# Attention and feed-forward on one core: the first pass over the keys begins with half of them, and projection blocks are cut in pieces of two matmuls

## The chip, the cores and the metric

The kernel runs on one NeuronCore of one Trainium2 chip. The metric is the device time of one execution in microseconds (us); each kernel is timed in several runs, and the median is given. A profile comes from one execution of its own.

## The reference, cut to what matters

Two sequences (B = 2) of T = 1024 rows of width D = 512 go through attention with 32 query heads and 8 key/value heads of width 16, a residual and a layer norm, then through a gated feed-forward of width 1408, a residual and a second layer norm. All is float32.

```python
Q = (x @ Wq.T + bq).reshape(b, t, HQ, HD).transpose(0, 2, 1, 3)
K = (x @ Wk.T + bk).reshape(b, t, HKV, HD).transpose(0, 2, 1, 3)
V = (x @ Wv.T + bv).reshape(b, t, HKV, HD).transpose(0, 2, 1, 3)
Q, K = _rope(Q, K)
K, V = jnp.repeat(K, G, axis=1), jnp.repeat(V, G, axis=1)
scores = jnp.einsum('bhqd,bhkd->bhqk', Q, K) / np.sqrt(HD)
w = jax.nn.softmax(scores, axis=-1)
attn = jnp.einsum('bhqk,bhkd->bhqd', w, V)
x = layernorm(x + attn.transpose(0, 2, 1, 3).reshape(b, t, D) @ Wo.T + bo)
out = layernorm(x + (silu(g) * u) @ down_w.T * down_s)      # g, u: gate and up of x
```

## The kernel before, in words

**Units and passes.** A unit `u` is one sequence `b`, one half `qh` of its queries (512) and one key head `g` with its four query heads; there are 32 units. Each unit is worked in eight steps. **Pass A** (`max_pass`, L325) multiplies queries by keys and takes each row's maximum: one step is one tile `t` of 128 queries against one half of 512 keys, for four heads. For each head two matmuls (`QH` and `QL`, the high and low part of the query) fill one PSUM bank, and VectorE reduces it to a column of `mx` (L341). When the eight steps of a unit are through, `max_rows` sends the maxima through DRAM into `mt`. **Pass B** (`exp_pass`, L362) forms the scores again, transposed, adds the negated maximum by a third matmul, and ScalarE takes the exponential (L378); `av` (L389) multiplies by V.

**Lead and loop.** Pass A runs LEAD = 12 steps ahead of pass B. These twelve steps stand alone in a first loop, called the lead below (`for n in range(LEAD)`, L623). After it comes the main loop over `c`, two steps of each pass a turn. The order of its instructions is written out by hand in three lists: `WITH_FILL` starts with `F`, which takes one item from the list `fill` and issues it; `NO_FILL` has no such item. While the first sequence's units run, `fill` holds 22 items, one a turn: two and four Q blocks of the first sequence, and sixteen items for the second sequence. After them turns run with `NO_FILL` until the projection and feed-forward items of the first quarter of rows become due, at turn c = 35. Those due turns are counted in c, not in time.

**A projection block.** `qk_block(b, half, m)` (L235) makes 128 columns of Q or K (m = 4 is K) for 512 rows: four program matmuls, which the profile records as eight, into one bank. Then ScalarE adds the bias (`q`, L256), GpSimd multiplies by the cosine (`t1`, L258), VectorE swaps the halves of each head (`rot`, a stream shuffle, L261), and `rot` times the sine, the sum, the high part and the low part follow (L262 to L265). With `fast=True` these are on VectorE and ScalarE and follow at once; otherwise GpSimd does them, one step later by `after(1, rest)`, and the two stores to DRAM are issued two steps after that. `rot` and `t1` have one buffer each. `prep(u)` (L310) loads a unit's keys `KS` and queries `QH`, `QL` back from DRAM. Each engine, and SyncE's queue of transfers, takes its instructions in the order of the program here (`tc.manual_schedule()`, L607).

**The start.** Eight tiles of x are loaded, then weights. Four tiles are turned by `x_turn` (L221), the rotation tables by `rope_turn` (L200, whose first instruction copies the table out to `rep` on VectorE, L203), then the other four tiles. Then come K of both halves, the first Q block, V of both halves (L292, L299), `prep(0)` and `prep(1)`, and the lead:

```python
qk_block(0, 0, D // P, fast=True)
qk_block(0, 1, D // P, fast=True)
qk_block(0, 0, 0, fast=True)
for half in range(NH):
    v_block(0, half)
prep(0)
prep(1)
```

One more Q block is issued whole in the lead, at n = 2 (L632). PSUM has four banks for pass A (`ps_a0`) and four for all else (`ps_q`) up to the end of the lead.

Of the kernel before, what the change touches and what calls it, by code (L numbers as in the profile page):

```python
# [7 lines left out]
F32 = mybir.dt.float32  # L8
I32 = mybir.dt.int32
F32R = mybir.dt.float32r  # L10
# [6 lines left out]
P = 128  # L17
B, T, D = 2, 1024, 512
HQ, HKV, HD = 32, 8, 16
G = HQ // HKV  # L20
E = 32
INTER = 1408
NT = T // P
# [3 lines left out]
QK = D + HKV * HD  # L27
KV = D + HKV * HD
HALF = 512
NH = T // HALF  # L30
TH = HALF // P
# [15 lines left out]
def attn_ffn_kernel(tc, x, wqkv, bqkv, wo, bo, rope, wg, wu, wd, gs, us, ds, out):  # L47
    nc = tc.nc
# [9 lines left out]
    ap3 = pool("ap3", 3)  # L58
    ap4 = pool("ap4", 4)
    wp = pool("wp", RING, side="right")  # L60
    qp1 = pool("qp1", side="right")
# [7 lines left out]
    def bank(name, shape=(P, HALF)):  # L69
        p, tag = psf[0]  # L70
        return p.tile(list(shape), F32, tag=tag, name=name)
# [8 lines left out]
    rope_sb = qp1.tile([P, NT, 2, HD], F32, name="rope_sb")  # L80
# [3 lines left out]
    def load_x(b, t):  # L84
        if b == 0:
            if t % TH == 0:
                XS["first"] = ap3.tile([P, TH, D], F32, tag="prob", name="xs0")
            XS[b, t] = XS["first"][:, t % TH, :]
        else:
            XS[b, t] = qp4.tile([P, D], F32, tag="xs", name="xs")  # L90
        nc.sync.dma_start(out=XS[b, t], in_=x[b, t * P : (t + 1) * P, :])

    def load_wqkv(n0, n1):
        nc.sync.dma_start(out=wqkv_sb[:, :, n0:n1], in_=wqkv[:, :, n0:n1])

    nc.sync.dma_start(out=rope_sb, in_=rope)
    for t in range(TH):
        load_x(0, t)
    for t in range(TH, NT):
        load_x(0, t)  # L100
    load_wqkv(D, KV)
    nc.sync.dma_start(out=bcol, in_=bqkv[:, 0:QK].rearrange("o (m p) -> p (o m)", p=P))
    load_wqkv(0, P)
    load_wqkv(KV, W)
    nc.sync.dma_start(out=bv_sb, in_=bqkv[:, KV:W].to_broadcast([P, W - KV]))
    load_wqkv(P, D)
# [19 lines left out]
    qT, kT = [], []  # L126
# [68 lines left out]
    XT, QB = {}, {}  # L195
    swap = [(i ^ (HD // 2)) for i in range(E)]
    cosT = qp1.tile([P, T], F32, name="cosT")
    sinT = qp1.tile([P, T], F32, name="sinT")

    def rope_turn():  # L200

        rep = qp1.tile([P, NT * 2, P // HD, HD], F32, name="rep")
        nc.vector.tensor_copy(  # L203
            rep,
            rope_sb.rearrange("p t s d -> p (t s) d")
            .unsqueeze(2)
            .to_broadcast([P, NT * 2, P // HD, HD]),
        )
        for i, tab in enumerate((cosT, sinT)):
            for half in range(NH):  # L210
                pt = bank("pt")
                for t in range(TH):
                    row = rep[:, (half * TH + t) * 2 + i, :, :]
                    nc.tensor.transpose(
                        pt[:, t * P : (t + 1) * P],
                        row.rearrange("p h d -> p (h d)"),
                        ident,
                    )
                nc.scalar.copy(tab[:, half * HALF : (half + 1) * HALF], pt)
# [15 lines left out]
    def qk_block(b, half, m, c0=0, c1=NC, fast=False):  # L235

        if c0 == 0:
            QB["p"] = bank("pq")
        pq = QB["p"]
        for c in range(c0, c1):  # L240
            nc.tensor.matmul(  # L241
                pq,
                wqkv_sb[:, c, m * P : (m + 1) * P],
                XT[b, half][:, c, :],
                start=c == 0,
                stop=c == NC - 1,
            )
        if c1 < NC:
            return
        ns = slice(half * HALF, (half + 1) * HALF)  # L250
        q = qp2.tile([P, HALF], F32, tag="q", name="q")
        rot = qp1.tile([P, HALF], F32, tag="rot", name="rot")
        t1 = qp1.tile([P, HALF], F32, tag="t1", name="t1")
        hi = qp2.tile([P, HALF], F32R, tag="hi", name="hi")
        lo = qp2.tile([P, HALF], F32R, tag="lo", name="lo")
        nc.scalar.activation(q, pq, AF.Identity, bias=bcol[:, m : m + 1])  # L256
        e = nc.vector if fast else nc.gpsimd
        nc.gpsimd.tensor_tensor(t1, q, cosT[:, ns], ALU.mult)  # L258

        def rest():  # L260
            nc.vector.stream_shuffle(rot, q, swap)  # L261
            e.tensor_tensor(rot, rot, sinT[:, ns], ALU.mult)  # L262
            e.tensor_tensor(t1, t1, rot, ALU.add)
            (nc.scalar.copy if fast else nc.gpsimd.tensor_copy)(hi, t1)
            e.tensor_tensor(lo, t1, hi.bitcast(F32), ALU.subtract)  # L265

        def store():
            for i, h in enumerate((hi, lo)):
                if m == D // P:
                    nc.sync.dma_start(  # L270
                        out=kT[b].rearrange("(p r) n -> p r n", r=2)[:, i, ns], in_=h.bitcast(F32)
                    )
                else:
                    nc.sync.dma_start(
                        out=qT[b][half, i, m * 2 * P : (m + 1) * 2 * P, :].rearrange(
                            "(p r) n -> p r n", r=2
                        ),
                        in_=h.bitcast(F32).unsqueeze(1).to_broadcast([P, 2, HALF]),
                    )

        if fast:
            rest()
            store()
        else:
            after(1, rest)
            after(3, store)

    def v_block(b, half):
        pv = bank("pv", (P, TH, HKV * HD))
        for t in range(TH):  # L290
            for c in range(NC):
                nc.tensor.matmul(  # L292
                    pv[:, t, :],
                    XT[b, half][:, c, t * P : (t + 1) * P],
                    wqkv_sb[:, c, KV:W],
                    start=c == 0,
                    stop=c == NC - 1,
                )
        nc.vector.tensor_tensor(  # L299
            vas[b][:, half * TH : (half + 1) * TH, :, :, 0],  # L300
            pv.rearrange("p t (g d) -> p t g d", d=HD),
            bv_sb.rearrange("p (g d) -> p g d", d=HD).unsqueeze(1).to_broadcast([P, TH, HKV, HD]),
            ALU.add,
        )
# [2 lines left out]

    KS, QH, QL, MX = {}, {}, {}, {}

    def prep(u):  # L310
        b, qh, g = UNITS[u]
        KS[u] = ap3.tile([P, T], F32R, tag="KS", name="KS")
        QH[u] = ap3.tile([P, HALF], F32R, tag="QH", name="QH")
        QL[u] = ap3.tile([P, HALF], F32R, tag="QL", name="QL")
        for j in range(G):
            nc.sync.dma_start(
                out=KS[u][j * E : (j + 1) * E, :].bitcast(F32), in_=kT[b][g * E : (g + 1) * E, :]
            )
        for i, op in enumerate((QH[u], QL[u])):
            nc.sync.dma_start(out=op.bitcast(F32), in_=qT[b][qh, i, g * P : (g + 1) * P, :])  # L320

# [2 lines left out]

    def max_pass(n, j, i):  # L325
        u, s = divmod(n, US)
        t, half = divmod(s, NH)
        if u not in MX:
            MX[u] = ap2.tile([P, TH, G, NH], F32, tag="mx", name="mx")
        r = slice(j * E, (j + 1) * E)  # L330
        if i == 0:
            PA[n, j] = ps_a[0].tile([P, HALF], F32, tag="pa", name="pa")
        nc.tensor.matmul(  # L333
            PA[n, j],
            (QH, QL)[i][u][r, t * P : (t + 1) * P],
            KS[u][r, half * HALF : (half + 1) * HALF],
            start=i == 0,
            stop=i == 1,
        )
        if i == 1:  # L340
            nc.vector.tensor_reduce(MX[u][:, t, j, half : half + 1], PA.pop((n, j)), AX.X, ALU.max)  # L341
# [233 lines left out]
        after(1 if q == LASTQ else 2 if now[0] >= STEPS else 5, store)  # L575


    fill = [lambda a=(0, half, m): qk_block(*a) for half, m in ((0, 2), (0, 3))]
    fill += [lambda m=m: qk_block(0, 1, m) for m in range(QK // P - 1)]

    def two_turns(t):
        for i in (t, t + 1):
# [8 lines left out]
    fill = [(0, f) for f in fill]  # L591
# [18 lines left out]
    for t in range(TH):  # L610
        x_turn(0, t)
    rope_turn()
    for t in range(TH, NT):
        x_turn(0, t)
    qk_block(0, 0, D // P, fast=True)
    qk_block(0, 1, D // P, fast=True)
    qk_block(0, 0, 0, fast=True)
    for half in range(NH):
        v_block(0, half)
    prep(0)  # L620
    prep(1)
    ps_a = [ps_a0]
    for n in range(LEAD):  # L623
        now[0] = n - LEAD
        for a in "0a 1a 0b 1b 2a 3a 2b 3b".split():
            max_pass(n, int(a[0]), "ab".index(a[1]))
        for f in later.pop(now[0], ()):
            f()
        if n % US == US - 1:
            max_rows(n // US)  # L630
        if n == 2:
            qk_block(0, 0, 1)  # L632
        if n == 7:
            prep(2)
    for t in range(4):
# [28 lines left out]
    for c in range(STEPS // 2):  # L664
# [11 lines left out]
        for s in NO_A if alone else WITH_FILL if has_fill else NO_FILL:  # L676
# [7 lines left out]
            n = 2 * c + int(s[-1])  # L684
# [5 lines left out]
            j, i = int(s[1]), "abc".index(s[2])  # L690
# [7 lines left out]
        u, s = divmod(2 * c + 1, US)  # L698
# [4 lines left out]
        if c == QS // 2 - 6:  # L703
# [9 lines left out]
                out=wd_sb.bitcast(F32), in_=wsd[2 * NF : PIECES].rearrange("f p n -> p f n")  # L713
# [159 lines left out]
```

## Time and profile before

| | us |
|---|---|
| median of three runs (lowest to highest) | 1245.93 (1244.38 to 1246.58) |
| time of the profiled execution | 1244.49 |
| its span | 1242.4 |
| TensorE busy | 1170.1 (94%) |
| VectorE busy | 872.4 (70%) |
| ScalarE busy | 704.7 (57%) |
| GpSimd busy | 354.1 (29%) |
| first matmul of pass A starts at | 38.10 |
| first block of the main loop starts at | 74.03 |

The span is the time from the first to the last instruction on the profiler's clock, and all places in time below are counted from its start. "Busy" counts the time in which an engine has an instruction in work; a matmul's end is modelled. The granted clock is the share of TensorE's full clock. The mean clock of the whole execution is 0.969.

### The profile page before, as it was taken

To read this page: it belongs to the slowest core of one execution; us is meant where nothing else is said; L and a number is where in the kernel's file an instruction comes from. 1 tells how busy PE (TensorE), PEld (TensorE's weight loads), DVE (VectorE), ACT (ScalarE), POOL (GpSimd) and SP (SyncE) were. 2 spreads that over 40 slices of the span, in tenths; PEclk is the share of its full clock that TensorE was granted. 3 is DMA by queue.
4 is the path that set the end of the run, shared out by engine and by line. 5 is a ranking of instruction groups with operands and counts; after the bars stand their busy time and mean duration, and the time that the engine had idled before them with its cause. 6 is when DMAs were issued, how large, how long until landed. Compare 5 with 4: busy or idle time off the path is not lost.

```text
span 1242.4 us, 22712 instructions
## 1 busy us (share of the span) xinstructions
PE 1170.1 (94%) x8784; PEld 606.5 (49%) x8784; DVE 872.4 (70%) x1492; ACT 704.7 (57%) x1300; POOL 354.1 (29%) x340
## 2 busy tenths in 40 slices
PE   7799999999799999999999999999999999999876
PEld 5344435454344454545444454546444454455664
DVE  4578898878677878785568878784867878703324
ACT  2026757566555766765446676763547776762350
POOL 3126351530103222224421222225331222245321
PEclk9679999999899999999999999999999999999897
DMA  5457776433411222221312222221212222111420
GB/s 159 130 190 252 249 233 237 155 132 122 135 44 61 79 79 81 93 78 52 99 48 67 82 92 84 84 78 44 79 60 87 78 78 79 45 61 43 136 60 36
DMA packets 82291, 126.80 MB, mean 102 GB/s; under 512 B 15873, under 2 KB 29442, under 8 KB 82050
## 3 DMA queue, kind: packets, MB, share of 16 engines
q1 hardware_dynamic: 82178, 125.30, 31.6%
q8 instruction: 71, 1.16, 0.4%
q14 instruction: 42, 0.34, 0.1%
HBM read 80.43 MB, written 36.44 MB: 94 GB/s over the span
## 4 chain that ended last, share of the span: by engine, by line
PE 62%; DVE 21%; POOL 5%; DMA 4%; issue 3%; ACT 3%; SPq 1%; POOLq 0%; DVEq 0%; ACTq 0%
PE pb L370 14%; PE pv L389 13%; DVE mx L341 12%; PE pa L333 11%; PE pg L504 10%; PE pq L241 5%; PE pd L546 5%; PE py L463 3%; DVE den L417 3%; POOL z L532 1%; DVE st L448 1%; DMA fl<-red 1%; POOL xq L561 1%; POOL ys L560 1%; DVE z L523 1%
## 5 line engine op out<-in xcount | busy, mean ns | idle before, releaser
L341 DVE TENSOR_REDUCE mx<-pa 128x1 f32<-128x512 f32 x1024 | 643.2, 681 | 187.8 <-PE pa L333 185.6
L378 ACT ACTIVATE prob<-pb 128x512 f32<-128x512 f32 x1024 | 544.5, 599 | 274.1 <-PE pb L370 263.0
L333 PE MATMUL pa<-KS,QH 32*128 32x512 f32 x1024 | 365.8, 470 | 41.7 <-DVE mx L341 23.8
L333 PE MATMUL pa<-KS,QL 32*128 32x512 f32 x1024 | 349.1, 432 | 0.0
L370 PE MATMUL pb<-QH,KS 32*128 32x512 f32 x1024 | 321.7, 477 | 1.0 <-ACT prob L378 1.0
L389 PE MATMUL pv<-prob,va 128*32 128x512 f32 x2048 | 275.5, 610 | 0.0
L370 PE MATMUL pb<-QL,KS 32*128 32x512 f32 x1024 | 270.6, 423 | 0.0
L370 PE MATMUL pb<-mt,ones 32*128 32x512 f32 x1024 | 254.5, 395 | 0.0
L333 PEld LDWEIGHTS pa<-KS,QH 32*128 32x128 f32 x1024 | 154.0, 186 | 168.7 <-DVE mx L341 144.2
L532 POOL TENSOR_TENSOR z<-pus,z 128x512 f32<-128x512 f32 x44 | 56.2, 1277 | 462.7 <-ACT pus L529 462.7
L370 PEld LDWEIGHTS pb<-QH,KS 32*128 32x128 f32 x1024 | 134.9, 182 | 82.5 <-issue 48.9
L370 PEld LDWEIGHTS pb<-QL,KS 32*128 32x128 f32 x1024 | 125.6, 184 | 85.6 <-issue 85.5
L333 PEld LDWEIGHTS pa<-KS,QL 32*128 32x128 f32 x1024 | 163.3, 188 | 5.4 <-DMA QL<-qT 0.5
L370 PEld LDWEIGHTS pb<-mt,ones 32*128 32x128 f32 x1024 | 140.6, 184 | 23.7 <-issue 15.9
L504 PE MATMUL pg<-x1h,wt 128*128 128x512 f32 x352 | 146.5, 416 | 0.7 <-ACT x1h L493 0.7
L504 PE MATMUL pg<-x1l,wt 128*128 128x512 f32 x352 | 139.5, 396 | 0.3 <-DVE x1l L494 0.3
L389 PEld LDWEIGHTS pv<-prob,va 128*32 128x32 f32 x2048 | 40.8, 108 | 93.9 <-issue 82.7
L504 PEld LDWEIGHTS pg<-x1h,wt 128*128 128x128 f32 x352 | 67.1, 191 | 38.0 <-issue 12.8
L546 PE MATMUL pd<-wd_sb,hh 128*128 128x512 f32 x176 | 71.8, 408 | 10.8 <-ACT hh L534 10.2
L241 PE MATMUL pq<-xT,wqkv_sb 128*128 128x512 f32 x160 | 76.7, 626 | 0.0
L504 PEld LDWEIGHTS pg<-x1l,wt 128*128 128x128 f32 x352 | 67.2, 191 | 13.1 <-DVE x1l L494 0.8
L546 PE MATMUL pd<-wd_sb,hl 128*128 128x512 f32 x176 | 70.5, 401 | 0.2 <-DVE hl L535 0.2
(80 smaller groups left out, 976.5 us busy)
## 6 DMA issues: line engine op xcount, KB each, us to landing
wt<-wsd SPq DMA_DIRECT2D x88, 256.0 KB
KS<-kT SPq DMA_DIRECT2D x128, 128.0 KB
wsd<-sr SPq DMA_DIRECT2D x33, 256.0 KB
qT<-hi SPq DMA_DIRECT2D x16, 512.0 KB
qT<-lo SPq DMA_DIRECT2D x16, 512.0 KB
QH<-qT SPq DMA_DIRECT2D x32, 256.0 KB
QL<-qT SPq DMA_DIRECT2D x32, 256.0 KB
xs<-in_x_dram SPq DMA_DIRECT2D x16, 256.0 KB
```

Of the source, the lines that this page charges most:

```text
L241: nc.tensor.matmul(pq, wqkv_sb[:, c, m * P : (m + 1) * P], XT[b, half][:, c, :], start=c == 0, stop=c == NC - 1,)
L333: nc.tensor.matmul(PA[n, j], (QH, QL)[i][u][r, t * P : (t + 1) * P], KS[u][r, half * HALF : (half + 1) * HALF], start=i == 0, stop=i == 1,)
L341: nc.vector.tensor_reduce(MX[u][:, t, j, half : half + 1], PA.pop((n, j)), AX.X, ALU.max)
L370: nc.tensor.matmul(PB[n, j], ones[r, :] if i == 2 else KS[u][r, kc * P : (kc + 1) * P], (QH[u], QL[u], mts[u % 2])[i][r, :], start=i == 0, ...
L378: nc.scalar.activation(prob[:, j, :], PB.pop((n, j)), AF.Exp, scale=SCALE)
L389: nc.tensor.matmul(PV[u][j * E : (j + 1) * E, :], vas[b][:, kc, g, :, :].rearrange("p d o -> p (d o)"), prob[:, j, :], start=done == 0, st ...
L417: after(min(k + 1, TH - 1), lambda ns=ns: nc.vector.reciprocal(den[:, ns], den[:, ns]))
L448: nc.vector.bn_stats(st, row)
L463: nc.tensor.matmul(py, NUM[q, c][:, t * P : (t + 1) * P], wo_sb[:, c, :], start=c == 0, stop=c == NC - 1,)
L504: nc.tensor.matmul(p, w[:, c, :], x1[:, c, :], start=c == 0 and k == 0, stop=c == NC - 1 and k == 1,)
L532: nc.gpsimd.tensor_tensor(z, pus, z, ALU.mult)
L546: nc.tensor.matmul(pd, h[:, f, t * P : (t + 1) * P], wd_sb[:, f, :], start=f == 0 and k == 0, stop=f == NF - 1 and k == 1,)
```

## The change

The second four tiles of x are loaded after the first weights. `rep` is copied before anything else on VectorE. The K block of the first half and the first Q block are issued right after `rope_turn`, ahead of the second four tiles; `prep` can load half of the keys, and the first unit's keys are loaded in two halves. Pass A takes all four query tiles against the first half of the keys, then against the second. V of the first half stays ahead of the lead; V of the second half and four Q blocks (one of them stood whole at n = 2 before, three stood in `fill`) are cut in two pieces each, and one piece is issued after each of the steps n = 1 to n = 10 of the lead. `fill` has 19 items in place of 22.

```diff
     for t in range(TH):
         load_x(0, t)
-    for t in range(TH, NT):
-        load_x(0, t)
     load_wqkv(D, KV)
     nc.sync.dma_start(out=bcol, ...)
     load_wqkv(0, P)
+    for t in range(TH, NT):
+        load_x(0, t)
     load_wqkv(KV, W)
...
+    rep = qp1.tile([P, NT * 2, P // HD, HD], F32, name="rep")
+    nc.vector.tensor_copy(rep, ...)
     def rope_turn():
-        rep = qp1.tile([P, NT * 2, P // HD, HD], F32, name="rep")
-        nc.vector.tensor_copy(rep, ...)
...
-    def v_block(b, half):
-        pv = bank("pv", (P, TH, HKV * HD))
-        for t in range(TH):
+    def v_block(b, half, t0=0, t1=TH):
+        if t0 == 0:
+            QB["v"] = bank("pv", (P, TH, HKV * HD))
+        pv = QB["v"]
+        for t in range(t0, t1):
...
+        if t1 < TH:
+            return
         nc.vector.tensor_tensor(
...
-    def prep(u):
+    def prep(u, n0=0, n1=T):
         b, qh, g = UNITS[u]
-        KS[u] = ap3.tile([P, T], F32R, tag="KS", name="KS")
+        if n0 == 0:
+            KS[u] = ap3.tile([P, T], F32R, tag="KS", name="KS")
+        for j in range(G):
+            nc.sync.dma_start(
+                out=KS[u][j * E : (j + 1) * E, n0:n1].bitcast(F32),
+                in_=kT[b][g * E : (g + 1) * E, n0:n1],
+            )
+        if n0 > 0:
+            return
...
         u, s = divmod(n, US)
-        t, half = divmod(s, NH)
+        half, t = divmod(s, TH)
...
-    fill = [lambda a=(0, half, m): qk_block(*a) for half, m in ((0, 2), (0, 3))]
-    fill += [lambda m=m: qk_block(0, 1, m) for m in range(QK // P - 1)]
+    fill = [lambda m=m: qk_block(0, 1, m) for m in range(1, QK // P - 1)]
...
     rope_turn()
+    qk_block(0, 0, D // P, fast=True)
+    qk_block(0, 0, 0, fast=True)
+    prep(0, 0, HALF)
     for t in range(TH, NT):
         x_turn(0, t)
-    qk_block(0, 0, D // P, fast=True)
     qk_block(0, 1, D // P, fast=True)
-    qk_block(0, 0, 0, fast=True)
-    for half in range(NH):
-        v_block(0, half)
-    prep(0)
+    prep(0, HALF, T)
     prep(1)
+    v_block(0, 0)
+    beside = [lambda a=(0, 0, 1, c): qk_block(*a, a[3] + 2) for c in (0, 2)]
+    beside += [lambda a=(0, 1, t): v_block(*a, a[2] + 2) for t in (0, 2)]
+    for half, m in ((0, 2), (0, 3), (1, 0)):
+        beside += [lambda a=(0, half, m, c): qk_block(*a, a[3] + 2) for c in (0, 2)]
...
-        if n == 2:
-            qk_block(0, 0, 1)
+        if n > 0 and beside:
+            beside.pop(0)()
```

More of the change, by code (lines that the diff above doesn't have):

```diff
@@ L198, in attn_ffn_kernel @@
     sinT = qp1.tile([P, T], F32, name="sinT")
-    def rope_turn():
-        rep = qp1.tile([P, NT * 2, P // HD, HD], F32, name="rep")
[L203 to L208, printed above, removed]
+    rep = qp1.tile([P, NT * 2, P // HD, HD], F32, name="rep")
+    nc.vector.tensor_copy(
+        rep,
+        rope_sb.rearrange("p t s d -> p (t s) d")
+        .unsqueeze(2)
+        .to_broadcast([P, NT * 2, P // HD, HD]),
+    )
+    def rope_turn():
         for i, tab in enumerate((cosT, sinT)):
@@ L308, in attn_ffn_kernel @@
     KS, QH, QL, MX = {}, {}, {}, {}
-    def prep(u):
+    def prep(u, n0=0, n1=T):
         b, qh, g = UNITS[u]
-        KS[u] = ap3.tile([P, T], F32R, tag="KS", name="KS")
+        if n0 == 0:
[4 more added lines that the diff above has]
+                in_=kT[b][g * E : (g + 1) * E, n0:n1],
+            )
+        if n0 > 0:
+            return
         QH[u] = ap3.tile([P, HALF], F32R, tag="QH", name="QH")
         QL[u] = ap3.tile([P, HALF], F32R, tag="QL", name="QL")
[L315 to L318, printed above, removed]
         for i, op in enumerate((QH[u], QL[u])):
```

## The prediction

> **What bounds the kernel now.** I read the slices first (TensorE at nine tenths nearly everywhere, seven only in the first slice, with DMA idle in between), then the windows of the first 100 us, the chain of waits over them, and the timeline of VectorE. The windows answer, ten us a row:
>
> ```profile
> core 0: us, PE busy (x) PEld busy (x) DVE busy (x) ACT busy (x) POOL busy (x), PEclk, DMA share, GB/s
> 20.00:30.00 10.00, 10.00 (x62) 7.51 (x61) 7.63 (x12) 2.94 (x5) 2.54 (x2) 1.00 0.30 107
> 30.00:40.00 10.00, 3.56 (x24) 2.30 (x22) 2.24 (x4) 0.09 (x1) 0.00 (x0) 0.80 0.90 262
> 40.00:50.00 10.00, 9.65 (x24) 4.98 (x23) 7.02 (x12) 0.00 (x0) 0.00 (x0) 0.52 0.18 53
> 50.00:60.00 10.00, 8.44 (x33) 4.11 (x31) 7.91 (x15) 0.69 (x1) 5.67 (x5) 0.82 0.02 8
> 60.00:70.00 10.00, 9.74 (x34) 6.06 (x32) 9.86 (x20) 0.00 (x0) 0.00 (x0) 0.50 0.28 101
> ```
>
> From 30 to 40 nothing computes while DMA is 90% busy; from 60 to 70 VectorE is full (9.86) and TensorE's 9.74 is at half clock, so it is waiting dressed as work. The chain of waits names the pieces (start, length, what; many left out):
>
> ```profile
> 34.47 3.59 DMA QH<-qT
> ...
> 45.90 5.50 PE pq L241 x8
> ...
> 55.23 9.55 DVE mx L341 x16
> ...
> 74.10 5.06 PE pq L241 x8
> ```
>
> So the end of the chain is set here by a round trip to DRAM, by two whole blocks at half clock, and between them by the reductions, 0.60 us apart (16 in 9.65). VectorE starts them at 39.75 and the main loop's first follows at 79.86. Two turns of that loop, the first with a Q block, the second without:
>
> ```profile
> 114.60:123.50 8.90, 8.90 (x68) 3.88 (x69) 7.80 (x12) 6.45 (x12) 5.73 (x5) 1.00 1.05 335
> 279.20:285.10 5.90, 5.90 (x58) 3.04 (x56) 5.01 (x9) 4.37 (x8) 0.00 (x0) 1.00 0.00 1
> ```
>
> TensorE is full in both: a block in the loop is paid in time. The starting times of the exponentials give 8.87 us for a turn with a Q block and (297.68 - 273.01) / 4 = 6.17 without.
>
> [...] idle from 31.7, clock 0.99 in 34 to 36 and 0.50 in 36 to 38; the block at 45.83 has its weight loads 0.85 apart at first and 0.43 from 49.95 on. [...] `q` of the second block waits from 21.1 to 21.67 behind `hi` of the first. [...] Here a `rot` product takes 1.10 to 1.29 beside GpSimd and the sum alone 0.69, while reductions keep 0.60 with GpSimd 5.67 of 10 us busy.
>
> **The start, step by step.** These VectorE lines set its pace:
>
> ```profile
> 9.20 1.22 DVE L203 COPY rep<-rope_sb 128x2048 f32<-128x2048 f32 x1
> ...
> 22.41 0.72 DVE L261 STREAM_SHUFFLE rot<-q 128x512 f32<-128x512 f32 x1
> 23.17 1.29 DVE L262 TENSOR_TENSOR rot<-rot,sinT 128x512 f32<-128x512 f32 x1
> 24.56 0.69 DVE L263 TENSOR_TENSOR t<-t,rot 128x512 f32<-128x512 f32 x1
> ```
>
> 1. `rep` moves to a time when VectorE is idle (its first work is at 6.78). The table transposes follow at 8.56, not 10.56, and end at 10.5. The first K block starts there, not at 14.09: 3.6 earlier. Its weights must be in: 1.7 MB ahead of them at some 300 GB/s from 2 us on gives 7.7, so they are. The four x tiles moved past three issues of SyncE (0.68 + 0.66 + 0.6) land near 11.5 and are first used at 17.4; the V weights, now behind them, near 13 and are used after 25. Cost nothing.
> 2. K and Q run their chains one after the other, 4.15 us each (shuffle 22.41 to shuffle 26.56): the second low part ends at 26.63 - 3.6 = 23.1.
> 3. The second x tiles are transposed from 17.4 to 19.4, but their copies to SBUF stand behind those chains: ScalarE's after `hi` (22.4), VectorE's after the low part. Two of 0.69 end at 24.5. This is a **new wait**: TensorE, and all of pass A behind it in order, waits from 19.4 to 24.5, long enough for half clock.
> 4. K of the second half costs 3.45 at full clock and 5.57 cold (the row at 45.83). I take cold, ending at 30.1; warm is 28.0. V of one half is 7.31 / 2 = 3.65, ending at 33.7.
> 5. The second K's chain ends 4.8 after its last matmul (17.6 to 22.49 for the first), at 34.9; V's 0.69 follows, and the first reduction starts at 35.6 (33.5 warm). `QH` is no longer last: stores at 22.4 and 23.1 plus the 7.3 from store to matmul of before, with 0.25 MB less to read, give at most 30.4. Against 39.75: **4.1 earlier**. The second half of the keys is stored by 35 and needed at n = 4, ten us later.
>
> **The lead.** On VectorE: 48 reductions of 0.605 (29.0), maxima 0.8, four shuffles of 0.73 (one before), one V addition 0.7: 33.4. On TensorE a piece is 1.74 and a step of pass A 0.75 (51.33 to 52.08) at full clock, 2.5 together, against 2.4 to 3.1 on VectorE: the two pace each other and four banks hide the hand-over. I add 2 for it. After V, TensorE is sparse again for some 4 us, so the first piece or two may run cold, 1.5 to 2.5 each: bounds 0 and 5, taken 1. The last reduction then ends at 35.6 + 36.4 = 72.0, against 75.2. The first block of the loop, warm, costs 3.45 in place of 5.06 and leaves VectorE a gap of 3.0 in place of 4.64: 75.0 against 79.86. So start and lead give **4.9**, though the lead carries three more Q blocks and half of V: they take the place of the 5.08 that VectorE idles from 47.02 to 52.09, and of cold clock.
>
> GpSimd needs 5.7 for a block (four of about 1.27, one of 0.61) and gets one every two steps, 5.2 to 5.6 here. It falls a little behind. Its lateness reaches VectorE only through `rot`: a shuffle must wait for the sum before it, due 3.3 after the last shuffle. Price 0, at most 2 per block and 6 in all if it queues. SyncE's stores of the third block wait for GpSimd near the end of the lead, and the loads of the second sequence and of weights wait behind them; first needed at turns 2 and 3, 15 us on: 0.
>
> **The loop.** Three items fewer: 3 × (8.87 - 6.17) = **8.1**. Its turns with reciprocals take 10.2, not all of which a shorter list removes: bounds 6 and 10. Due turns are counted in c, so all later work comes earlier by the same amount. Pass A's order within a unit changes no count in the loop: 0, the keys there being loaded long ahead.
>
> **Sum.** 4.9 + 8.1 = 13.0 off the profiled execution's 1244.49 (span 1242.4) gives 1231.5. It is the lowest region of three runs around 1245.93; off that median it is 1232.9. I take 1232.5.
>
> **Rivals.** About 2.5 us (0.2%) is what the measurement can tell from no change.
> - *As summed*: 8 to 18 gained, 0.60.
> - *Warm throughout*: K starts before the clock falls (2.1), no cold pieces (1), hand-overs free (2), the loop's 10: gain 18 to 20, near 1226. [...] Chance 0.12.
> - *The new wait moves further*: GpSimd queues up to 6, or cold pieces cost their 5, and half of the gain goes: 2.5 to 8 gained, near 1240. For it: GpSimd is at its limit on paper. Chance 0.16.
> - *Slower*: the clock stays at half in the lead. Then a piece costs 3.4 (four of 0.85) and a step of pass A 1.5, 4.9 for 2.8, over ten steps 21 lost and 13 gained: 1254. It turns to loss when more than six of ten pieces run cold. For it: the clock was 0.5 in the old lead. Against: TensorE had little to do there, while pieces keep it near full, which restored the clock within 4 us at 45.83. Chance 0.09.
> - *No gain*: first reduction no earlier and turns without an item no shorter than those with one. The two loop rows speak against it. Chance 0.03.
>
> Faster 0.60 + 0.12 + 0.16 = 0.88, same 0.03, slower 0.09. The range reaches from the warm case, 1226, to inside the third, 1241.
>
> **What would show it.** In the profile after: K's first matmul near 10.5; x copies behind the chains and TensorE idle from about 19 to 24; first reduction at 33 to 36; clock near 1.0 from n = 3 of the lead on; the loop's first reduction near 75; 19 turns with an item. I am wrong if pieces run with weight loads 0.85 apart in most of the lead, if shuffles wait for GpSimd's `rot`, or if turns 19 to 21 take over 8 us.

## The result, and the profile after

The changed kernel takes 1237.16 us in the median of four runs (1236.38 to 1239.19), the kernel before 1245.21 beside it: ratio 0.9937, 95% interval 0.992 to 0.9954. That is 8.0 us off, where 13 were forecast. The profiled execution took 1236.51 with a span of 1234.4. Measured a second time, the ratio was 0.9938 (0.992 to 0.9955).

The windows of the changed kernel, in the same columns as before the change:

```profile
core 0: us, PE busy (x) PEld busy (x) DVE busy (x) ACT busy (x) POOL busy (x), PEclk, DMA share, GB/s
20.00:30.00 10.00, 6.25 (x15) 3.14 (x16) 2.81 (x5) 2.05 (x4) 0.00 (x0) 0.66 0.57 179
30.00:40.00 10.00, 7.89 (x46) 5.00 (x46) 8.59 (x14) 0.85 (x2) 1.27 (x1) 0.90 0.30 94
40.00:50.00 10.00, 10.00 (x62) 5.73 (x61) 7.26 (x13) 0.69 (x1) 2.97 (x3) 0.93 0.30 97
50.00:60.00 10.00, 10.00 (x46) 4.47 (x46) 9.09 (x17) 0.69 (x1) 3.97 (x4) 1.00 0.29 107
60.00:70.00 10.00, 9.36 (x30) 3.42 (x27) 7.85 (x16) 0.69 (x1) 7.94 (x7) 0.83 0.22 65
```

The hole has moved from 30:40 to 20:30 and is smaller; from 40 to 60 TensorE is full with the clock at 0.93 and 1.00, where the kernel before had 0.52 and 0.82. From 60 to 70 VectorE falls to 7.85 and the clock to 0.83. The chain of waits (start, length, what):

```profile
23.75 5.71 PE pq L242 x8
...
34.95 2.40 DVE mx L350 x4
...
65.37 3.61 PE pq L242 x4
...
80.12 6.16 issue
```

The first line is K of the second half at half clock, as forecast (0.50 from 23.75 to 26). The third is a piece of two matmuls that took 3.6 instead of 1.9, at a clock of 0.54 (65.3 to 69). The last is new: 6.16 us in which the chain finds no work at all ("issue"). The timelines of GpSimd, SyncE and VectorE, one after the other, explain it:

```profile
86.33 0.30 POOL L122 TENSOR_SCALAR gs<-gst 128x11 f32<-128x11 f32 x1 [6.20 <-DMA gst<-in_gs_dram]
86.59 1.28 POOL L259 TENSOR_TENSOR t<-q,cosT 128x512 f32<-128x512 f32 x1
```

```profile
72.36 0.63 SPq L275 DMA_DIRECT2D qT<-lo  x1
...
78.79 0.34 SPq L120 DMA_DIRECT2D gst<-in_gs_dram  x1
```

```profile
90.48 0.01 DVE L262 LOAD_MASK_SELECT rot<-q  x1 [3.36 <-POOL t L264]
```

GpSimd stands 6.20 us at an instruction that halves a gate scale (`gs2`, in `load_weights`). That scale's load is issued only at 78.79, behind four stores of the lead's Q blocks (the last at 72.36) and the larger loads after them, and lands at 86.3. The next Q block's products queue behind it, and VectorE's shuffle, with all reductions behind it, waits 3.36 for `rot`. So turn 1 of the main loop (start of its `q` to that of turn 2) takes 98.72 - 85.21 = 13.5 us:

```profile
85.20:98.70 13.50, 10.71 (x68) 4.31 (x72) 9.33 (x16) 5.95 (x11) 11.85 (x11) 0.87 0.74 238
```

### The profile page after: what moved, and what is told of

It reads as the page before. It is cut to its first block, busy times and chain, and to the rows that moved or that the text cites. A ratio compares the mean times of both kernels' runs of the same rounds, so it can differ in the third digit from the quotient of the medians.

```text
span 1234.4 us, 22718 instructions
## 1 busy us (share of the span) xinstructions
PE 1163.5 (94%) x8784; PEld 599.8 (49%) x8784; DVE 875.8 (71%) x1492; ACT 705.3 (57%) x1300; POOL 352.8 (29%) x340
## 4 chain that ended last, share of the span: by engine, by line
PE 63%; DVE 20%; POOL 6%; issue 4%; ACT 4%; DMA 3%; SPq 0%; POOLq 0%; DVEq 0%; ACTq 0%
PE pb L379 14%; PE pv L398 13%; DVE mx L350 11%; PE pa L342 11%; PE pg L513 10%; PE pq L242 5%; PE pd L555 5%; PE py L472 3%; DVE den L426 3%; POOL z L541 1%; DVE st L457 1%; DMA fl<-red 1%; POOL xq L570 1%; POOL ys L569 1%; PE pv L295 1%
## 5 line engine op out<-in xcount | busy, mean ns | idle before, releaser
L342 PE MATMUL pa<-KS,QH 32*128 32x512 f32 x1024 | 352.3, 458 | 38.1 <-DVE mx L350 27.1
L342 PE MATMUL pa<-KS,QL 32*128 32x512 f32 x1024 | 336.5, 421 | 0.0
L342 PEld LDWEIGHTS pa<-KS,QH 32*128 32x128 f32 x1024 | 147.8, 182 | 163.9 <-DVE mx L350 145.1
L342 PEld LDWEIGHTS pa<-KS,QL 32*128 32x128 f32 x1024 | 158.5, 184 | 4.9
L242 PE MATMUL pq<-xT,wqkv_sb 128*128 128x512 f32 x160 | 81.2, 650 | 4.9 <-DVE xT L232 4.9
L555 PE MATMUL pd<-wd_sb,hh 128*128 128x512 f32 x176 | 71.9, 408 | 10.8 <-ACT hh L543 10.2
```

What stands on the lines that cost most here:

```text
L242: nc.tensor.matmul(pq, wqkv_sb[:, c, m * P : (m + 1) * P], XT[b, half][:, c, :], start=c == 0, stop=c == NC - 1,)
L342: nc.tensor.matmul(PA[n, j], (QH, QL)[i][u][r, t * P : (t + 1) * P], KS[u][r, half * HALF : (half + 1) * HALF], start=i == 0, stop=i == 1,)
L555: nc.tensor.matmul(pd, h[:, f, t * P : (t + 1) * P], wd_sb[:, f, :], start=f == 0 and k == 0, stop=f == NF - 1 and k == 1,)
```

## The experiments

Each ratio is to the kernel before, run beside it on the same chip; 0.001 is 1.25 us. Rows 2 to 5 come from one chip, `whole_gs` to `best` from a second, the last three and the repetition of the changed kernel from a third, so differences between kernels are differences of ratios. Every kernel below `before_gs_late` has the edit of `gs_late` too. The two right columns are places in the profile, in us.

| kernel | ratio (95%) | first reduction | loop's first reduction |
|---|---|---|---|
| changed, first / again | 0.9937 / 0.9938 | 34.87 | 77.28 |
| `gs_late` | 0.9892 (0.9873 to 0.9911) | 35.78 | 78.03 |
| `before_gs_late` | 0.9999 (0.9986 to 1.0012) | 40.59 | 81.86 |
| `refill_gs` | 0.9950 (0.9932 to 0.9968) | 35.63 | 75.40 |
| `tmajor_gs` | 0.9916 (0.9900 to 0.9931) | 36.42 | 82.46 |
| `whole_gs` | 0.9980 (0.9968 to 0.9992) | 36.22 | 87.41 |
| `piece0_gs` | 0.9881 (0.9858 to 0.9903) | 34.66 | 77.36 |
| `xfirst_gs` | 0.9907 (0.9882 to 0.9932) | 36.15 | 77.97 |
| `best` | 0.9900 (0.9877 to 0.9922) | 37.54 | 79.49 |
| `xsplit_gs` | 0.9877 (0.9859 to 0.9895) | 32.41 | 75.69 |
| `pieces12_gs` | 0.9892 (0.9869 to 0.9916) | 35.71 | 74.47 |
| `best2` | 0.9874 (0.9855 to 0.9893) | 32.30 | 71.27 |

**The wait for the gate scale.** `gs_late`:

```diff
     def load_weights():
-        nc.gpsimd.tensor_scalar(gs2, gst, 0.5, None, ALU.mult)
...
     load_weights()
+    later.setdefault(40, []).append(
+        lambda: nc.gpsimd.tensor_scalar(gs2, gst, 0.5, None, ALU.mult)
+    )
```

> The changed kernel with the doubling of the gate scale (gs2, one GpSimd instruction of 0.3 us, whose result is first used after turn 35) issued at step 40 of the loop instead of right after the lead. Theory QUEUE: in the changed kernel this instruction waits for the transfer gst (6.2 us idle on GpSimd, to 86.33), the next Q block's GpSimd work waits behind it, VectorE's shuffle waits 3.36 for that, and turn 1 takes 13.5 us in place of 8.9. Then it gains about 4.6: 1232.5, and turn 1 falls to about 8.9. Rival TRANSFERS: turns 0 to 2 are slow because the transfers are full there (357 and 316 GB/s from 70 to 90 us); then 1237, as the changed kernel. Rival CLOCK: turn 1 is slow because TensorE's clock fell; then 1237 too.

`before_gs_late` has the same edit on the kernel before.

> The kernel before with the same instruction issued at step 40. QUEUE: there GpSimd's work for the next block started at 84.84, late but with no shuffle waiting for it, so nothing is gained: 1245 within 1, and the stall of the changed kernel is one that the change uncovered. If the instruction cost the kernel before as much, it would gain 4 to 5: 1241.

`gs_late` stands at 0.9892, 5.7 us below the changed kernel, with intervals that do not meet; turn 1 falls to 94.85 - 85.98 = 8.87 us. The kernel before gains nothing by the same edit. (The instruction multiplies by 0.5, so it halves the scale.) VectorE's timeline of `gs_late` has the shuffle of turn 1 with no wait:

```profile
87.82 0.73 DVE L261 STREAM_SHUFFLE rot<-q 128x512 f32<-128x512 f32 x1
```

So it is QUEUE. The transfers were as full in `gs_late` (313 to 373 GB/s from 70 to 95 us) and turn 1 did not mind them; the clock, 0.77 from 90 to 95 in the changed kernel, stayed at 1.00 there, so its fall followed from the stall. The stall is one that the change uncovered.

**The moved blocks.** `refill_gs` puts three Q blocks back into the loop's list.

```diff
-    for half, m in ((0, 2), (0, 3), (1, 0)):
-        beside += [...]
-    fill = [lambda m=m: qk_block(0, 1, m) for m in range(1, QK // P - 1)]
+    fill = [lambda a=(0, half, m): qk_block(*a) for half, m in ((0, 2), (0, 3))]
+    fill += [lambda m=m: qk_block(0, 1, m) for m in range(QK // P - 1)]
```

> gs_late with the three Q blocks back in the list of the main loop (22 items), so that the lead has pieces only at n = 1 to 4. Theory: three turns lengthen from 6.2 to 8.9 (+8.1), the lead loses three shuffles (2.2) and the hand-overs and the cold piece of n = 5 to 10 (about 2 to 3): net 3 to 4 slower than gs_late, 1236. Rival: a block costs as much in the lead as in the loop; then as gs_late. Rival: the lead's second fall of the clock comes from the maxima alone and stays; then 5 to 6 slower than gs_late.

7.2 us slower than `gs_late`, more than any case expected, though 5 to 6 lies inside the two intervals. The lead is 2.6 shorter (75.40 against 78.03). At the copy of the sixth unit's output the kernel is 283.82 - 276.57 = 7.25 behind, so in this pair of profiles the three blocks cost 9.9 in the loop.

Other pairs give less. From the loop's first reduction to that copy, the three kernels with 22 items (the kernel before, `before_gs_late`, `refill_gs`) take 208.4 to 208.7 us; the seven with 19 items and no stall take 198.5 to 203.8. So three blocks are worth 4.6 to 10.2, in the middle about 8. Part of the spread is the clock: between the fourth and the fifth unit's copy the changed kernel takes 33.21 and `gs_late` 31.59, with a clock of 0.57 from 246 to 250 in the first and of 1.00 at the same place (242 to 246) in the second, though no edit reaches there.

**The order of the keys.** `tmajor_gs`:

```diff
-        half, t = divmod(s, TH)
+        t, half = divmod(s, NH)
```

> gs_late with pass A in the old order (both halves of the keys for one query tile, then the next tile), all else as changed. Theory: the second half of the keys is then needed at n = 1 instead of n = 4; its stores are issued at 33.65 and 34.38 and its loads at 36.88, so n = 1 waits until about 40 instead of starting at 36 to 37: 2.5 to 4 slower than gs_late. Rival: VectorE works through the second K block ahead of the first reduction in any case, so the order of the keys gives nothing: as gs_late within 1.

3.0 us slower by the ratios, though the intervals overlap; the trace is plainer. VectorE waits for the second half of the keys (TensorE stands 5.09 us, to 40.33, for a transfer of `KS`) and then 3.49 beside the first piece, which ran cold by an estimate from that wait (in `gs_late` the wait there is 2.63, with the clock at 0.50 from 40 to 42):

```profile
41.71 2.48 DVE L349 TENSOR_REDUCE mx<-pa 128x1 f32<-128x512 f32 x4 [2.82 <-PE pa L341]
47.69 5.06 DVE L349 TENSOR_REDUCE mx<-pa 128x1 f32<-128x512 f32 x8 [3.49 <-PE pa L341]
```

From first reduction to loop it needs 46.04 against 42.25. So half of the keys first is worth about 3.8 in the lead of these profiles.

**The pieces.** `whole_gs` issues each block of the lead whole, at the step of its second piece:

```diff
-    beside = [lambda a=(0, 0, 1, c): qk_block(*a, a[3] + 2) for c in (0, 2)]
-    beside += [lambda a=(0, 1, t): v_block(*a, a[2] + 2) for t in (0, 2)]
+    idle = lambda: None
+    beside = [idle, lambda: qk_block(0, 0, 1), idle, lambda: v_block(0, 1)]
...
-        beside += [lambda a=(0, half, m, c): qk_block(*a, a[3] + 2) for c in (0, 2)]
+        beside += [idle, lambda a=(0, half, m): qk_block(*a)]
```

> gs_late with the blocks of the lead whole instead of in pieces: V after step n = 4, the Q blocks after n = 2, 6, 8 and 10. Theory: a whole block is 3.6 us on TensorE at full clock and the four banks hold 2.4 us of reductions, so VectorE stands idle 1.5 to 2 us at each of five blocks, and 2 more at the first, at half clock; the pieces' own gaps (0.2 to 0.5 each) go: 4 to 7 slower than gs_late. Rival: the pieces give nothing, since VectorE's idle time then only gathers in one place: as gs_late within 1.

11 us slower than `gs_late`, where 4 to 7 were expected: four fifths of what `gs_late` gains. From first reduction to loop it needs 51.19 against 42.25. TensorE's timeline, in which a warm block takes 3.7, and VectorE's longest waits:

```profile
42.28 5.99 PE L241 MATMUL pq<-xT,wqkv_sb 128*128 128x512 f32 x8
...
59.88 5.40 PE L241 MATMUL pq<-xT,wqkv_sb 128*128 128x512 f32 x8
...
69.18 3.70 PE L241 MATMUL pq<-xT,wqkv_sb 128*128 128x512 f32 x8
...
76.78 5.40 PE L241 MATMUL pq<-xT,wqkv_sb 128*128 128x512 f32 x8
```

```profile
48.96 2.48 DVE L349 TENSOR_REDUCE mx<-pa 128x1 f32<-128x512 f32 x4 [5.49 <-PE pa L341]
...
65.98 2.48 DVE L349 TENSOR_REDUCE mx<-pa 128x1 f32<-128x512 f32 x4 [4.42 <-PE pa L341]
...
82.87 2.48 DVE L349 TENSOR_REDUCE mx<-pa 128x1 f32<-128x512 f32 x4 [3.79 <-PE pa L341]
```

Three of four Q blocks run cold (5.99 and twice 5.40 where the warm one takes 3.70; the clock is 0.66 from 40 to 50, 0.83 from 60 to 70 and 0.88 from 70 to 80); the expectation counted one. VectorE's gaps in the lead sum to 16.9, against 7.6 in `gs_late`. The three cold blocks run 5.7 over the warm 3.70, the two cold pieces of `gs_late` 2.4 over the warm 1.98 (3.4 in the changed kernel: 3.67 and 3.68). So the clock makes some 2 to 3 of the 9.3, an estimate from these durations; the greater part is VectorE idle while a whole block runs.

**The cold first piece.** `piece0_gs`:

```diff
-        if n > 0 and beside:
+        if beside:
```

> gs_late with the pieces issued after the steps n = 0 to 9 instead of 1 to 10. Theory CLOCK: the first piece ran at half clock (3.6 us, VectorE idle 2.6) because TensorE had only two reductions' worth of matmuls per 2.4 us for some four us before it; with a piece right after n = 0 it stays at full clock (1.9 us a piece) and the gap of 2.6 closes to under 1: 1.5 to 2.5 faster than gs_late. Rival: the gap is the hand-over of the banks and not the clock; then it only moves, as gs_late within 0.7.

0.9881 against 0.9892: not to be told apart. VectorE's gap ahead of n = 2 stayed at 2.65, so CLOCK as I put it failed: the piece after n = 0 ran warm (1.98), but the next was cold (3.54). TensorE's timeline of `piece0_gs`, and its windows at the fall:

```profile
33.41 1.98 PE L241 MATMUL pq<-xT,wqkv_sb 128*128 128x512 f32 x4
35.40 1.09 PE L341 MATMUL pa<-KS,QH 32*128 32x512 f32 x2
...
37.85 3.54 PE L241 MATMUL pq<-xT,wqkv_sb 128*128 128x512 f32 x4
```

```profile
36.00:38.00 2.00, 1.90 (x8) 0.91 (x9) 2.00 (x4) 0.00 (x0) 0.00 (x0) 1.00 0.16 23
38.00:40.00 2.00, 2.00 (x3) 0.81 (x4) 1.53 (x3) 0.00 (x0) 0.00 (x0) 0.53 0.59 178
```

TensorE is "busy" 1.90 of 2.00 ahead of the fall. For the 2.4 us from 35.40 it had only pass A's narrow matmuls at VectorE's pace: eight, which the kernel before does in 0.75 where nothing holds them up (51.33 to 52.08). The clock then fell, and no run shows whether their pace was the cause. At the other end, after the two steps left without a piece, the loop's first block ran cold (6.36, where the changed kernel takes 3.70; VectorE idle 5.26).

**The copies of x.** `xfirst_gs` moves `x_turn` of the second four tiles between the first K block and the first Q block.

> gs_late with the second four tiles of x turned between the first K block and the first Q block, so that their copies to SBUF no longer stand behind the first Q block's chain. Theory: K of the second half then runs from about 19.5 to 23 at full clock instead of 24 to 29.5; the first reduction comes when QH and QL have landed, near 32 instead of 35: 2 to 3.5 faster than gs_late. Rival: the first Q block's chain gets 1.3 later and with it QL, and half clock moves to the wait for it; nothing is gained: as gs_late within 0.7.

No gain: the rival's result, by another way. A transpose's bank was the next that the Q block needed, and its copy stood behind K's `hi` on ScalarE, so the Q block started 2.9 late and with it QL. TensorE's timeline:

```profile
19.37 7.13 PE L241 MATMUL pq<-xT,wqkv_sb 128*128 128x512 f32 x16 [2.89 <-ACT xT L233]
...
34.50 0.73 PE L341 MATMUL pa<-KS,QH 32*128 32x512 f32 x2 [4.42 <-DMA QH<-qT]
```

`best` puts this, `gs_late`, pieces from n = 0 and a cast on ScalarE together.

> All together: gs_late, the second x tiles turned ahead of the first Q block, pieces from n = 0, and the cast of the first unit's negated maxima on ScalarE (on VectorE it took 1.29 us beside GpSimd's product, in place of 0.18). If the parts add: 2 to 3.5 and 1.5 to 2.5 and 1 off gs_late, 5 to 7 faster, about 19 under the kernel before. If the waits stand in series behind one thing (QL's landing), 3 to 4 faster than gs_late.

0.9900, no better than `gs_late`; it keeps the bank wait (2.88) and starts at 37.54. The maxima with their cast take 1.26 there in place of 1.96. `xsplit_gs` takes the bank wait away:

```diff
-    qk_block(0, 0, 0, fast=True)
-    prep(0, 0, HALF)
-    for t in range(TH, NT):
-        x_turn(0, t)
+    prep(0, 0, HALF, queries=False)
+    qk_block(0, 0, 0, 0, NC - 1)
+    psf[0] = (ps_a0, "pa")
+    for t in range(TH, NT):
+        x_turn(0, t)
+    psf[0] = (ps_q, "pf")
+    qk_block(0, 0, 0, NC - 1, NC, fast=True)
+    prep(0, 0, 0)
...
```

`prep` gets a switch for this (left out here), so that it can load keys without queries; its last use above loads the queries alone.

> gs_late with the x copies between the two chains as in xfirst_gs, but with three of the first Q block's four matmuls ahead of the x transposes, the transposes in pass A's free banks (so that no matmul waits for a bank, which cost xfirst_gs 2.9 us), and the loads of the first half of the keys issued ahead of the Q stores (2.9 us of SyncE off QL's way). Theory: the first reduction then comes near 31 in place of 35, and the kernel is 3 to 4 faster than gs_late. Rival: the round trip of Q through DRAM is set by its bytes, so QL lands near 34 as before and nothing is gained: within 1 of gs_late.

The first reduction comes at 32.41, 3.4 earlier than in `gs_late`; it is now QL that ends the wait (1.06 at 31.59 on TensorE's timeline), so the theory and its rival are both right in part. By the loop 2.3 are left, and by the ratios nothing certain: 0.9877 against 0.9892. In its profile the third unit gives the 2.3 back: a reciprocal waits 0.97 for the transfer `den`, and the clock is 0.66 from 160 to 165.

**More pieces.** `pieces12_gs` has a fifth Q block in the lead and pieces from n = 0 to 11, with no item in turn 0; `best2` adds `xsplit_gs` to it.

```diff
-    for half, m in ((0, 2), (0, 3), (1, 0)):
+    for half, m in ((0, 2), (0, 3), (1, 0), (1, 1)):
...
-    fill = [lambda m=m: qk_block(0, 1, m) for m in range(1, QK // P - 1)]
+    fill = [lambda m=m: qk_block(0, 1, m) for m in range(2, QK // P - 1)]
...
-    fill = [(0, f) for f in fill]
+    fill = [(1, f) for f in fill]
```

> gs_late with a fifth Q block in the lead (twelve pieces, after n = 0 to 11), 18 items in the loop's list, and turn 0 without an item. Theory: one item less in the loop gives 2.7 to 3.3, one shuffle more costs 0.7, no cold block stands ahead of turn 0; the clock still falls once near n = 1, as in piece0_gs: 2 to 4 faster than gs_late. Rival: GpSimd, 5.7 us a block at one block every 5.5, queues and its shuffles wait: no gain.

> xsplit_gs and pieces12_gs together: if they add, 5 to 8 faster than gs_late, near 0.984 of the kernel before. If the pieces only fill the time that TensorE would have waited for QL, 3 to 4.

Both profiles are the shortest of all (spans 1228.8 and 1225.7), but the ratios, 0.9892 and 0.9874, do not stand clear of `gs_late`. What can be said is that `best2` beats the kernel before (0.9855 to 0.9893) and the changed kernel (0.9938, 0.9920 to 0.9955, on the same chip). Whether the two parts add is not shown.

> The changed kernel once more, beside the others of this call on one chip, so that their ratios can be set against its own: 0.9937 of the kernel before if the first measurement holds; gs_late stood at 0.9892.

It held: 0.9938, with the same wait for `gst` (6.07) and the shuffle's (3.20).

## Why the prediction was right, and where it was not

The direction and the range held. Its steps:

- **Start (steps 1 to 5), 4.1 forecast, 4.9 measured.** K's first matmul at 9.85 (10.5), the second low part's end at 22.40 (23.1), TensorE's wait for the x copies 4.91 (5.1), K of the second half cold at 5.70 (5.57), first reduction at 34.87 (35.6). `rep` was sized wrongly: 4.47 us, not 1.22. It ended at 7.40, past VectorE's first work of before (6.78), and TensorE waited 0.25 for an x copy behind it; no more of it shows. The weights of the first K block were in, as the estimate from 300 GB/s had it (the transfers moved 311 GB/s from 2 to 8 us in the kernel before). Half clock came within the wait for the copies: TensorE's last matmul ahead of it ended at 18.84, and the clock was 1.00 up to 21.0 and 0.50 from there, 2.2 us on. In the kernel before, the last matmul ended at 31.69, and the clock was 0.98 from 35.5 to 36 and 0.50 from there, 4.3 us on. So the two traces show no one length of idleness for the fall, and the chance of a warm K block was the author's estimate. One reading was loose: nothing computed from 32.4 to 38.1, not from 30 to 40.
- **The lead, 39.4 forecast from first reduction to loop, 42.4 measured.** VectorE's work is 34.7, not 33.4, mostly since one small cast took 1.29 in place of 0.18. Its gaps sum to 7.8 (2.69, 0.22, 0.40, 0.51, 2.05, 1.89), not 6.0. Two pieces ran cold, not one (3.67 and 3.68, where a warm one takes 1.98; clock 0.52 from 38 to 40 and 0.50 from 66 to 68): after n = 1, and after n = 9, when VectorE had spent 2.5 us on a shuffle and the unit's maxima. So start and lead gave 2.6, not 4.9.
- **The loop, 8.1 forecast, 3.7 measured** (from its first reduction to the sixth unit's copy: 208.46 before, 204.78 after). The three blocks are not the reason: with the 4.6 of turn 1 added back it is 8.3. The step that failed is one priced at nothing: "the loads of the second sequence and of weights wait behind them; first needed at turns 2 and 3, 15 us on: 0". It passed over `gs2`, which stands in GpSimd's queue at turn 0, ahead of the Q blocks' products. GpSimd's timeline of the kernel before:

```profile
84.58 0.30 POOL L122 TENSOR_SCALAR gs<-gst 128x11 f32<-128x11 f32 x1 [24.64 <-ACT prob L378]
...
87.41 1.28 POOL L263 TENSOR_TENSOR t<-t,rot 128x512 f32<-128x512 f32 x1
```

  There `gs2` ran 4.7 us after the loop's first reduction, the sum that frees `rot` ended at 88.69, and turn 1's shuffle started at 89.64 without a wait. (The view infers ScalarE as the releaser; the instruction reads `gst` alone.) In the changed kernel `gs2` runs 9.1 us after the loop's first reduction. Of these 4.3 us more, 2.6 are the earlier start of the loop and 1.7 the later run of `gs2`. The load took 7.5 us from issue to use, and at most 7.9 before (76.64 to 84.58). From 70 to 90 us 6.73 MB are moved, against 4.75 before; how much of the delay is the load's place in the queue and how much are these bytes, no run separates. By the sixth unit's copy (282.06, against 288.32) start, lead and loop have given 6.3.
- **The rest.** The gain is 7.8 at the seventh unit's copy, 5.9 at the eighth and 6.5 at the last (1125.31 to 1118.85); the final 1.5 of the span's 8.0 come after it. So some 6 us are accounted for, and about 2 came where no edit reaches. Why is open. The later part of the kernel moved by 1 to 3 us between profiled executions of these kernels without an edit that reaches it, and this blurs all small effects here.
- **The rivals.** The gain of 8.0 lies where the sum (8 to 18) and the third case (2.5 to 8) meet. By its mechanism it is the third: GpSimd's queue, and the shuffle that waits for `rot`, which the prediction had named as a sign that it is wrong. But the queue's cause was a load, not GpSimd's own work, which it got through. The other two signs stayed away: two of ten pieces were cold, and turns 19 to 21 took some 6 to 7 us. That the gain came out at the sum's edge and not further down is luck, as far as the 2 us go that no edit explains (without them it would be near 1239, still inside the range). The slower case (half clock through the lead) did not happen with pieces; in `whole_gs`, without them, three of four Q blocks ran cold (5.40 to 5.99 beside 3.70).

## What to carry to other kernels

When stores move ahead of loads in a queue, or the readers of these loads move earlier, follow each load to its first reader on every engine, the small constants too: 0.3 us of work with a late operand, in front of a queue that another engine waits for, cost 5.7 of the 13.5 us that the change gains without it. Work moved beside a stage that another engine bounds should be cut finely: here pieces left VectorE 7.6 us of gaps and whole blocks 16.9, by the estimate above for the most part through the length of a block and for some 2 to 3 us through the clock. Before moving a tile's copies forward, look which PSUM bank the next block gets: in `xfirst_gs` the Q block stood 2.89 for its bank.

## What the runs showed of the hardware that I had not expected

- Two copies on VectorE became several times longer beside GpSimd. VectorE's timeline of the changed kernel:

```profile
2.93 4.47 DVE L201 COPY rep<-rope_sb 128x2048 f32<-128x2048 f32 x1 [2.93 <-DMA rope_sb<-in_rope_dram]
...
60.46 1.29 DVE L359 CAST mm<-neg 128x16 fp32r<-128x16 f32 x1
```

  They took 1.22 and 0.18 in the kernel before, where GpSimd had nothing in work beside them (its memsets end at 6.32 and `rep` starts at 9.20; its product ends at 59.94 and the cast starts at 65.02). In the changed kernel the first runs beside GpSimd's memsets and ends 1.08 after the last of them (6.32); the second runs beside its product of 1.26 at 60.45 and ends with it (61.75 and 61.71). How the one lengthens the other is not shown.
- TensorE's clock fell without an idle gap that the profile names: in `piece0_gs`, 2.4 us of narrow matmuls at a third of their pace (0.75 in the kernel before) between two pieces came ahead of the fall (1.00 from 36 to 38, 0.53 from 38 to 40), with TensorE busy 1.90 of 2.00. In the changed kernel the same 2.4 us followed an idle gap of 1.91, and the clock was 0.52 from 38 to 40. The prediction had looked for idleness alone.
